# In the softmax step of pairs 5 and 0, the query tile with 128 keys is taken first of four instead of last

## Chip, core and metric

The kernel runs on one core of one Trainium2 chip, in one launch. The metric is the device time of that core in microseconds (us). All arithmetic of the kernel that matters here is 32-bit floating point.

## What is computed

One transformer block with modulation, for 2048 tokens of width 512. A causal attention with 16 heads of width 128 is followed by a mixture of 64 experts with 4 chosen for each token and two shared feed-forward units. Only the attention bears on the change:

```python
q = jnp.einsum('bpm,hmd->bphd', x, Q_w) + Q_b
k = jnp.einsum('bpm,hmd->bphd', x, K_w) + K_b
v = jnp.einsum('bpm,hmd->bphd', x, V_w) + V_b
logits = jnp.einsum('bqhd,bkhd->bhqk', q, k) / math.sqrt(d_head)
causal_mask = jnp.triu(jnp.ones((s, s), dtype=bool), k=1)
logits = jnp.where(causal_mask, NEG, logits)
scores = jax.nn.softmax(logits, axis=-1)
attn = jnp.einsum('bhqk,bkhd->bqhd', scores, v)
out = jnp.einsum('bqhd,hdm->bqm', attn, O_w) + O_b
```

Here `x` is the normalised and modulated input. The mask makes query tile number t (128 queries) need only the first (t+1)*128 keys, so the 16 query tiles of a head have widths from 128 to 2048 keys.

## The kernel before

**Steps.** The 16 query tiles of a head form 8 pairs: pair p holds the tiles 2p and 2p+1. `BATCHES` (L437) divides them into five steps s = 0 to 4: (7), (6), (5, 0), (4, 1), (3, 2). Steps 0 and 1 have two tiles each, steps 2, 3 and 4 have four. The list `steps` (L439) runs over all heads and steps, 80 in all. `tiles_of` (L450) gives the order of a step's tiles: in step 2 these are tile 11 (1536 keys), tile 1 (256), tile 10 (1408) and tile 0 (128).

**Softmax of one tile** (`softmax_tile`, L457). The tile is cut into chunks of at most 1024 keys. For each chunk `chunk` (L493) issues: matmuls of queries with keys into a PSUM tile `ps` (L500); on VectorE the causal mask on the last 128 columns of the tile (L512), the negated maximum (L513) and, for a second chunk, the minimum of both (L517); on ScalarE the exponential from `ps` into the probability tile `p`, with its row sum (L519, followed by an instruction that reads the accumulator), and for a second chunk a correction factor `fix` (L529). `ps` has two buffers (tag "sc" of the pool `psA`, L124), so a chunk's matmuls wait until the exponential of the chunk before the last one has read its buffer. The division by the sums, `normalise` (L471), is put off: it is flushed in the middle of the next chunk, or at the end of the step. In steps 2 to 4 its large part goes to ScalarE, after the next chunk's exponential (L714); in steps 0 and 1 it is done on VectorE (L487).

**From probabilities to values.** At a step's end `swap` (L727) flushes what was put off and issues 16 DMAs on SP's queue (L544), which move 32-row blocks of `p` to their transposed places in `pt`. Later VectorE transposes the 32x32 blocks in two halves (`turn`, L732, L554). Then TensorE multiplies with the values into a PSUM tile `po` (`weighted_values`, L572); every one of these matmuls reads both halves of `pt`. ScalarE adds the bias (`at`, L581), and GpSimd's queue stores the result (L586).

**The loop** (L746) runs over the 80 steps. Loop turn (hd, s) carries three streams, which `merge` (L83) interleaves by their share of work done: the softmax of the step two further on (first in the list, so it wins a tie), the weighted values of step s itself, and `fillers`: projections of the next head (`project`, L207, its matmuls at L217) in turns 0 to 2, values of the next group of heads (`make_v`, L419) in turns 3 and 4, and matmuls of the output (L688) in the last head. At 0.55 and 0.8 of the turn's work stand the two transposes for the next step:

```python
streams = [weighted_values(hd, s, turned.pop(n)), fill]
if n + 2 < len(steps):
    streams.insert(0, softmax_work(n + 2))
...
if n + 1 < len(steps):
    marks.append((0.55, lambda: turn(n + 1, 0)))
    marks.append((0.8, lambda: turn(n + 1, 1)))
merge([st for st in streams if st], marks)
if n + 2 < len(steps):
    swap(n + 2)
```

So the softmax of step 2 is worked on in loop turn (hd, 0); it follows on the softmax of step 1 in the turn before (of the head before), and the softmax of step 3 follows on it in turn (hd, 1). The order on each engine is the order of these calls; engines run their own instructions in order.

Of the kernel before, what the change touches and what calls it, by code (L numbers as in the profile page):

```python
# [23 lines left out]
def adaln_block_kernel(  # L24
# [96 lines left out]
    with ExitStack() as att:  # L121
# [328 lines left out]
        def tiles_of(s):  # L450

            prs = BATCHES[s]
            if len(prs) == 1:
                return [(prs[0], 1), (prs[0], 0)]
            return [(prs[0], 1), (prs[1], 1), (prs[0], 0), (prs[1], 0)]

        def softmax_tile(hd, s, pr, i, pb):  # L457
# [261 lines left out]
        def softmax_work(n):  # L719
            hd, s = steps[n]  # L720
            probs[n] = pp.tile([P, PW], F32, name="p")
            out = []
            for pr, i in tiles_of(s):
                out += softmax_tile(hd, s, pr, i, probs[n])
            return out
# [760 lines left out]
```

## Time and profile before

| what | us |
|---|---|
| three runs: lowest, median, highest | 2420.52, 2423.49, 2424.94 |
| the profiled execution: its time | 2422.97 |
| the profiled execution: its span, first to last instruction | 2421.2 |
| granted clock of TensorE, mean over the span | 0.996 of full speed |
| attention loop, about | 107 to 1695 of the span |
| one head, start of loop turn 0 to the next, heads 7 to 8 | 811.9 to 910.3 |
| DMAs that move `p` to `pt` (SP's queue): issue to landing, median | 2.2 |

Times of instructions that the change touches, as means over the kernel (ns): for a chunk of 128 keys the mask takes 290, the maximum 292, the exponential 363 and its read of the accumulator 194, the scaling by ScalarE 390. The mask and the maximum of a chunk of 384 keys take 290 and 558, its exponential 582; for 1024 keys the maximum takes 1213, the exponential 1115 and the scaling 1146. One half of a transpose takes 2242 for step 0, 1976 for step 1 and 1907 for steps 2 to 4.

A row of the timeline gives the start in the span, the time, the engine, the line, the operation, the tiles (output<-inputs), the shape and a count; consecutive instructions of a line are merged. In brackets stands how long the engine was idle before it, and which instruction released it. A matmul of the program makes two MATMUL records, each with a weight load on the row of PEld. The end of a MATMUL record includes its way through the array, so that at full flow the next one starts before it ends: records of 512 columns follow each other every 0.43 us, of 256 columns every 0.215, and the two of a 128-column matmul take 0.22 together.

### The profile page before, as it was taken

The numbers are of one execution on the slowest core, as the hardware profiler recorded it, in microseconds if no ns is written. First come the engines' busy times: TensorE is split into PE (matmuls) and PEld (weight loads), VectorE is DVE, ScalarE is ACT, GpSimd is POOL, SyncE is SP. The second block draws the span as 40 slices with busy tenths as digits, with TensorE's granted clock in tenths as the row PEclk, the third lists the DMA queues.
The fourth block names the chain that finished last, engine by engine and source line by source line (L and its number), as shares of the span: only waits on it lengthen the run. The fifth ranks groups of instructions, "written<-read, shape, count | busy, mean of one in ns | idle before, by whom it ended". The sixth has DMA issues, their size and how long they took to land. (4 is left out here: it accounts for less than half of the span.)

```text
span 2421.2 us, 26178 instructions
## 1 busy us (share of the span) xinstructions
PE 2362.5 (98%) x8406; PEld 1500.5 (62%) x8406; DVE 1513.2 (62%) x2878; ACT 829.8 (34%) x1737; POOL 219.2 (9%) x286
## 2 busy tenths in 40 slices
PE   7999999999999999999999999999999999999999
PEld 3566656666566665666656656555444476877743
DVE  5367666676676767767666666774655563654564
ACT  3243443444444444444444443432211221222200
POOL 0000000000000000000000000000000111111074
PEclk9999999999999999999999999999999999999999
DMA  4224444454454444444435445564432368877665
GB/s 139 64 71 116 120 118 109 98 143 102 101 127 105 117 120 96 114 111 103 112 93 129 110 99 120 164 194 134 152 122 87 98 203 246 236 217 240 191 194 158
DMA packets 223681, 325.22 MB, mean 134 GB/s; under 512 B 31876, under 2 KB 138424, under 8 KB 223544
## 3 DMA queue, kind: packets, MB, share of 16 engines
q1 hardware_dynamic: 196664, 252.21, 40.3%
q0 software_dynamic: 17664, 54.54, 7.5%
q10 hardware_dynamic: 9216, 16.78, 1.8%
q8 instruction: 68, 1.11, 0.2%
q14 instruction: 69, 0.57, 0.1%
HBM read 138.86 MB, written 41.94 MB: 75 GB/s over the span
## 5 line engine op out<-in xcount | busy, mean ns | idle before, releaser
L519 ACT ACTIVATE p<-ps,nm 128x1024 f32<-128x1024 f32 (+7 forms) x384 | 332.4, 866 | 885.1 <-DVE nm L517 403.9
L572 PEld LDWEIGHTS po<-pt,v 128*128 128x128 f32 x2304 | 426.5, 190 | 249.8 <-issue 187.8
L572 PE MATMUL po<-pt,v 128*128 128x256 f32 (+1 forms) x2304 | 572.3, 368 | 6.6 <-DVE pt L554 5.2
L500 PE MATMUL ps<-kt,qt 128*128 128x512 f32 (+3 forms) x1280 | 531.2, 531 | 20.9 <-ACT p L519 18.7
L513 DVE TENSOR_REDUCE nm<-ps 128x1 f32<-128x1024 f32 (+7 forms) x384 | 348.9, 909 | 48.9 <-PE ps L500 40.2
L554 DVE STREAM_TRANSPOSE pt<-pt 128x1664 f32<-128x1664 f32 (+2 forms) x160 | 318.0, 1988 | 56.3 <-DMA pt<-p 51.4
L500 PEld LDWEIGHTS ps<-kt,qt 128*128 128x128 f32 x1280 | 234.7, 190 | 180.9 <-issue 137.0
L427 PE MATMUL pv<-wv,hT 128*128 128x256 f32 x1024 | 240.8, 379 | 2.2 <-ACT v L434 2.2
L586 POOL DMA_DIRECT2D atd<-at x128 | 74.4, 584 | 1617.4 <-ACT at L581 1155.8
L427 PEld LDWEIGHTS pv<-wv,hT 128*128 128x128 f32 x1024 | 194.4, 190 | 31.2 <-ACT v L434 3.0
L714 ACT ACTIVATE p<-p,rs 128x1024 f32<-128x1024 f32 (+7 forms) x256 | 200.5, 807 | 6.2 <-DVE rs L475 5.9
L1056 PE MATMUL pso<-hT,T 128*128 128x512 f32 x384 | 174.8, 600 | 0.0
L217 PE MATMUL pqk<-T,sw 128*128 128x512 f32 x360 | 169.2, 592 | 0.0
L512 DVE TENSOR_TENSOR ps<-ps,causal 128x128 f32<-128x128 f32 x256 | 74.3, 290 | 150.0 <-PE ps L500 147.6
L1348 PE MATMUL pse<-wgu,xbT 128*128 128x256 f32 x512 | 121.1, 379 | 0.0
L1056 PEld LDWEIGHTS pso<-hT,T 128*128 128x128 f32 x384 | 70.1, 192 | 72.1 <-issue 71.3
L217 PE MATMUL pqk<-hT,wq 128*128 128x512 f32 x240 | 114.1, 598 | 0.0
L1265 PE MATMUL psd<-wsd,hs 128*128 128x512 f32 x256 | 111.5, 592 | 0.0
L1348 PEld LDWEIGHTS pse<-wgu,xbT 128*128 128x128 f32 x512 | 93.8, 190 | 11.7 <-issue 1.0
L217 PEld LDWEIGHTS pqk<-T,sw 128*128 128x128 f32 x360 | 68.3, 190 | 47.8 <-issue 43.0
L1331 POOL DMA_INDIRECT xb<-h2d,tok x64 | 65.2, 1018 | 301.8 <-PE tpx L1341 275.1
L1343 ACT COPY xbT<-tpx 128x512 f32<-128x512 f32 x64 | 37.4, 586 | 146.0 <-DVE y L1371 54.4
(365 smaller groups left out, 2344.3 us busy)
## 6 DMA issues: line engine op xcount, KB each, us to landing
pt<-p SPq DMA_DIRECT2D x768, 104.0 KB, 2.2
pt<-p SPq DMA_DIRECT2D x256, 124.0 KB, 2.3
pt<-p SPq DMA_DIRECT2D x256, 108.0 KB, 2.2
atd<-at POOLq DMA_DIRECT2D x128, 128.0 KB, 2.2
wgu<-in_L_ffn_Wg_dram SPq DMA_DIRECT2D x64, 256.0 KB, 4.6
wgu<-in_L_ffn_Wu_dram SPq DMA_DIRECT2D x64, 256.0 KB, 4.9
wd<-in_L_ffn_Wd_dram SPq DMA_DIRECT2D x64, 256.0 KB, 3.7
ybd<-y ACTq DMA_DIRECT2D x64, 256.0 KB, 3.8
```

Of the source, the lines that this page charges most:

```text
L217: nc.tensor.matmul(out=ps, lhsT=l[:, k], rhs=r[:, k], start=(k == 0), stop=(k == 1))
L427: nc.tensor.matmul(out=ps, lhsT=hTs[t // 4][:, k, (t % 4) * P : (t % 4 + 1) * P], rhs=wv[:, k].rearrange("p i d -> p (i d)"), start=(k == ...
L500: nc.tensor.matmul(out=ps[:, o : o + wo], lhsT=q, rhs=kts[hd, (c0 + o) // 512][:, :wo], start=True, stop=True,)
L513: nc.vector.tensor_reduce(nm[:, n : n + 1], ps[:, :w], AX.X, ALU.max, negate=True)
L519: nc.scalar.activation(rows[:, r0 + c0 // P : r0 + (c0 + w) // P], ps[:, :w].rearrange("q (r b k) -> q r b k", b=4, k=32), AF.Exp, bias=nm ...
L554: nc.vector.transpose(part, part)
L572: nc.tensor.matmul(out=po if wide else po[:, P:], lhsT=vts[g, kt // 4][:, kt % 4, hh * DH : (hh + 1) * DH], rhs=rows[:, r : r + last + 1 : ...
L586: nc.gpsimd.dma_start(out=atd[hd, :, o * 256 : (o + 1) * 256], in_=at[:, m])
L714: nc.scalar.activation(part, part, AF.Identity, scale=r)
L1056: nc.tensor.matmul(out=ps, lhsT=abs_[pr][:, hd, i * P : (i + 1) * P], rhs=wos[hd // 4][:, hd % 4, :], start=(hd == 0), stop=(hd == H - 1),)
L1265: nc.tensor.matmul(out=ps, lhsT=hsh[b, f][:, i * P : (i + 1) * P], rhs=wsd[:, f, :], start=(f == 0), stop=(f == NHC - 1),)
L1348: nc.tensor.matmul(out=ps, lhsT=xts[e][:, k, :], rhs=weights[e][:, k].rearrange("p i h -> p (i h)"), start=(k == 0), stop=(k == DC - 1),)
```

## The change

`tiles_of` gets a case of its own for the step whose second pair is pair 0:

```diff
             prs = BATCHES[s]
             if len(prs) == 1:
                 return [(prs[0], 1), (prs[0], 0)]
+            if prs[1] == 0:
+                return [(0, 0), (prs[0], 1), (0, 1), (prs[0], 0)]
             return [(prs[0], 1), (prs[1], 1), (prs[0], 0), (prs[1], 0)]
```

Step 2 of every head then takes its tiles in the order 0, 11, 1, 10. Its chunks had the widths 1024, 512, 256, 1024, 384, 128 and now have 128, 1024, 512, 256, 1024, 384. The places of the tiles in `p` and `pt` stay (`first_block`, L443), and so do all other steps. No instruction is added or removed; the merge spreads them otherwise. At the start of turn (hd, 0) TensorE's order was (512-column projections count two matmuls)

```
ps 1024 | po 256 | projection x2 | po x3 | projection x2 | po | ps 512 | po x2
```

and becomes

```
ps 128 | po 256 | projection x2 | ps 1024 | po x3 | projection x2 | po x2 | ps 512 | po
```

and at its end `ps 384 | po 256 | ps 128 | po 128`, followed by `ps 1024` of the next step, becomes `ps 384 | po 256 | po 128`, followed by the same. In the last head, whose filler is the output's matmuls, the 1024 chunk stands after one `po` and one such matmul. The order of SP's and GpSimd's instructions is the same as before. On ScalarE `at` (L581) stood between the scalings of tile 10 and of tile 0; it now stands ahead of the scalings of tile 10, which are the last before the swap.

## Prediction

> **What bounds the kernel now.** I read the page's busy shares first, then the list of who waited for whom on TensorE, then the timeline at the two places where the order changes.
>
> ```profile
> PE 2362.5 (98%) x8406; PEld 1500.5 (62%) x8406; DVE 1513.2 (62%) x2878; ACT 829.8 (34%) x1737; POOL 219.2 (9%) x286
> ```
>
> TensorE is busy 98% of the span and no matmul is added or removed, so the time can change only through TensorE's gaps. The waits of TensorE (total us, times, longest) name two kinds in the attention loop:
>
> ```profile
> PE ps L500 <- ACT p L519: 18.7, 18, 1.6
> PE po L572 <- DVE pt L554: 5.2, 4, 3.6
> ```
>
> Fifteen of the 18 waits of the first kind lie at one place, which I call border A: the start of loop turn (hd, 1), heads 0 to 14. In head 7 the timeline shows:
>
> ```profile
> 831.24 0.81 PE L500 MATMUL ps<-kt,qt 128*128 128x384 f32 x2
> ...
> 832.31 0.38 PE L500 MATMUL ps<-kt,qt 128*128 128x128 f32 x2
> ...
> 832.53 0.39 PE L572 MATMUL po<-pt,v 128*128 128x128 f32 x2
> ...
> 833.20 0.58 ACT L519 ACTIVATE p<-ps,nm 128x384 f32<-128x384 f32 x1 [3.29 <-DVE nm L517]
> ...
> 833.93 1.98 PE L500 MATMUL ps<-kt,qt 128*128 128x512 f32 x4 [1.01 <-ACT p L519]
> ```
>
> The two last chunks of step 2 (384 and 128 keys) are issued 1.07 us apart. The next chunk, 1024 keys of step 3, needs the buffer of the 384 chunk, and that is free only at 833.93, 0.15 after its exponential ends. Nothing else stands behind it that TensorE could do.
>
> The second place is border B, the start of turn (hd, 0), where the changed step begins. Before, in head 7:
>
> ```profile
> 809.84 2.24 DVE L554 STREAM_TRANSPOSE pt<-pt 128x1984 f32<-128x1984 f32 x1
> ...
> 811.88 1.88 PE L500 MATMUL ps<-kt,qt 128*128 128x512 f32 x4
> 812.00 0.27 DVE L512 TENSOR_TENSOR ps<-ps,causal 128x128 f32<-128x128 f32 x1
> ...
> 813.41 0.80 ACT L519 ACTIVATE p<-ps,nm 128x640 f32<-128x640 f32 x1 [3.12 <-DVE nm L517]
> 813.60 0.59 PE L572 MATMUL po<-pt,v 128*128 128x256 f32 x2
> ```
>
> The first po matmul needs the second transpose of pt, which ends at 812.08, **after** TensorE has entered the turn at 811.88. There is no wait, because the 1024 chunk lies between and covers 1.72 us. Where the transpose is later still, the wait shows (head 0, then head 13):
>
> ```profile
> 113.08 1.09 PE L572 MATMUL po<-pt,v 128*128 128x256 f32 x2 [3.63 <-DVE pt L554]
> ...
> 1403.92 0.70 PE L572 MATMUL po<-pt,v 128*128 128x256 f32 x2 [0.21 <-DVE pt L554]
> ```
>
> **Part 1, removed: the wait at border A.** With the new order the chunk before the last one has 1024 keys (tile 10); its exponential in head 7 ran from 828.31 to 829.42, over 3 us before TensorE reaches the border. The 384 chunk's buffer is wanted only by the second chunk of the turn, in head 7 at 841.34. The price of one wait: in full flow the 1024 chunk would have started 0.22 after 832.53, at 832.75; it started at 833.93, 1.18 late, and took 1.82 to the next row instead of 1.72, so 1.28 lost. The same over heads 0 to 14: 1.28, 1.80, 1.27, 1.51, 1.28, 1.28, 1.92, 1.28, 1.34, 1.27, 1.88, 1.32, 1.32, 1.75, 1.28. Sum **-21.8**. Head 15 has no such wait (its output matmuls lie between). Next in line at the border is the po matmul after the 1024 chunk; its transpose ended 0.5 to 1.3 before the border in all 15 heads, so nothing is late there.
>
> **Part 2, added: the transpose loses its cover at border B.** Now only a 128 chunk (0.22) stands ahead of the first po. Let S be the start of turn (hd, 0) and T the end of the second transpose. T - S in heads 1 to 14: 0.84, 0.47, 1.51, 0.99, 0.63, 0.45, 0.20, 1.38, 0.64, 0.87, 0.47, 1.65, 2.04, 0.94; sum 13.1. po starts 0.055 after T (head 13: 1403.87 to 1403.92) and its restart costs 0.10 (0.53 to the next row, where full flow has 0.43). So each head loses T - S + 0.055 - 0.22 + 0.10: 13.1 - 14 x 0.065 = 12.2. Off go the 0.47 and 0.09 that heads 13 and 12 lost there already: **+11.6**. Behind the waiting po on TensorE's queue stands everything, the projections and the 1024 chunk included; VectorE and ScalarE wait for these but are behind TensorE here anyway, still scaling step 1 until 816.38.
>
> **Part 3, the moved 1024 chunk.** It now needs the buffer of step 1's last chunk (640 keys). That exponential starts 1.33 after T, takes 0.80, and frees the buffer 0.15 later: T + 2.28. TensorE arrives at T + 0.055 + 0.53 + 1.72 = T + 2.305. A tie; a weight load is issued ahead of its matmul and waits with it, so I take one restart, 0.1 x 14 = **+1.4** (nothing at best; 0.3 each at worst).
>
> **Part 4, head 15 and head 0.** In head 15 T - S is 2.42 and only one po and one output matmul (0.86) stand ahead of the 1024 chunk. Lost: 2.42 - 0.065 = 2.36 for po, then T + 2.28 against T + 1.445 = 0.83 and a restart, less the 0.86 lost there now: **+2.4**. In head 0 both transposes stand ahead of the loop, and the 1024 chunk that TensorE did meanwhile now comes after: 1.72 - 0.22 = **+1.5**. [...] The row: the gap of 3.63 was followed by a granted clock of half speed,
>
> ```profile
> 110.00:115.00 5.00, 1.92 (x4) 1.23 (x5) 4.14 (x3) 0.78 (x1) 0.00 (x0) 0.83 0.76 176
> ```
>
> (the 0.83 is the clock; four projection records took 3.22 instead of 1.88). [...] The gap here becomes 5.1. [...]
>
> **Part 5, hidden.** The tile's own instructions (on VectorE 0.29 + 0.29 + 0.16, on ScalarE 0.36 + 0.19 + 0.39) move from the end to the start. At the start they lie behind step 1's scaling; the 1024 chunk's maximum moves from 816.29 to about 817.0, its exponential to about 818.3, and the buffers it frees are wanted after 822. If that cover were gone, 0.7 a head would show, 11 in all. At the end `at` now precedes tile 10's scaling on ScalarE; it needs the last po, done at about 833, and the scaling cannot start before 834.7 anyway. The swap's 16 DMAs on SP start about 3.2 after the 384 chunk's exponential starts (1.53 to the scaling, 1.66 for it), at 836.6 instead of 837.1: earlier on the clock, but 0.8 later against TensorE, which gained 1.28. They take 10.06 to issue and 2.2 to land, until about 848.9; the second transpose that needs them stood at 850.74, behind work that follows TensorE, and moves to 849.5. Covered, except in the five heads with the longest waits (0.1 to 0.2 each), where the wait behind it at turn (hd, 2) grows: **+0.5** (0 to 3).
>
> **Sum.** -21.8 + 11.6 + 1.4 + 2.4 + 1.5 + 0.5 = -4.4. Against the profiled execution's own 2422.97 (span 2421.2 and 1.8 around it) that gives 2418.6. The median of the runs is 0.5 above the profiled one, so 2419.
>
> **The rivals.** (a) *The full gain.* The transpose keeps its distance to TensorE rather than to the start of the turn, or the new waits are half as long: then -12 to -18, 2405 to 2411. For it: VectorE follows TensorE most of the time. Against: ahead of the second transpose VectorE is backed up (maximum, step 0's scaling of 1.28, transpose, with hardly a pause), and in heads 3 and 12 the first transpose waits some 2 us for its DMAs, so TensorE can't pull it. (b) *Slower: the wait at border B outgrows the one at A.* Place: the second transpose of step 0's pt. Price: 14 times the wait. It decides from a mean of about 1.25 a head at B, where I have 0.83 + 0.1. For it: the four latest heads (1.51, 1.65, 2.04, 2.42) have a mean of 1.9; if DMA arrivals were as late in every head, part 2 would be 14 x 1.84 = 25.8, and the whole about +10: 2433. Against: eight of the 14 stay under 0.9. (c) *It doesn't do what it says*: the 1024 chunk at border A meets another wait of the same size; then only the added parts count, +17: 2441. Against it stands the 3 us margin.
>
> **How the numbers follow.** Forecast (both waits trade, net -10 to +3) 0.63; (a) 0.15; (b) 0.19; (c) 0.03. Three runs spread 0.18%, so about 0.2%, 4.8 us, is what can be told from no change. The forecast's own range is 2413 to 2426, from parts 2 to 5 each at their ends; it sits just inside the 0.2%, and divides into 0.27 faster, 0.34 same, 0.02 slower. With (a) faster, (b) and (c) slower mostly and the same in some: 0.42, 0.36, 0.22. The range that should hold 8 in 10 reaches towards (a) and (b): 2410 to 2428.
>
> **What would show it.** Right: the list of waits has "ps <- ACT p" down from 18 entries to a few, none at border A, and "po <- DVE pt" up from 4 to about 16, some 15 us, all at the start of turn (hd, 0). Part 3 is wrong if ps waits at border B by more than 0.2. Part 5 is wrong if turn (hd, 2) opens with longer waits than now. The forecast falls if T - S has another mean than 0.9, or if a clock below 1.00 shows in the loop outside head 0.

## The result, and the profile after

The changed kernel takes 2420.05 us (median of 20 runs, 2418.85 to 2427.73) against 2425.63 for the kernel before (20 runs, 2420.52 to 2428.93). The ratio is 0.9982, with a 95% interval of 0.9976 to 0.9988: a small gain of 0.18%, some 4.4 us (2.9 to 5.8 by the interval; the two medians lie 5.6 apart). The profiled execution has a span of 2418.1 us.

The page's first row and the list of who waited on TensorE (total us, times, longest), after the change, whose lines are two further down in the file (L502 is L500 of before, L574 is L572, L556 is L554):

```profile
PE 2363.9 (98%) x8406; PEld 1500.2 (62%) x8406; DVE 1511.8 (63%) x2878; ACT 828.8 (34%) x1737; POOL 217.8 (9%) x286
```

```profile
PE po L574 <- DVE pt L556: 15.0, 12, 5.1
...
PE ps L502 <- ACT p L521: 4.0, 8, 0.9
```

The two waits have changed places: `ps` for the exponential fell from 18.7 to 4.0, `po` for the transpose rose from 5.2 to 15.0. The busy times of TensorE, VectorE and ScalarE are the same within 0.2%.

At border A (start of turn (hd, 1)) in head 7, the timeline after:

```profile
828.93 0.81 PE L502 MATMUL ps<-kt,qt 128*128 128x384 f32 x2
...
829.58 0.82 PE L574 MATMUL po<-pt,v 128*128 128x256 f32 x4
...
830.23 1.88 PE L502 MATMUL ps<-kt,qt 128*128 128x512 f32 x4
...
830.90 0.58 ACT L521 ACTIVATE p<-ps,nm 128x384 f32<-128x384 f32 x1 [3.29 <-DVE nm L519]
```

The next step's first chunk starts at 830.23, before the exponential of the 384 chunk has begun, and with no idle time. At border B (start of turn (hd, 0)), head 1:

```profile
210.80 2.24 DVE L556 STREAM_TRANSPOSE pt<-pt 128x1984 f32<-128x1984 f32 x1
...
211.72 0.39 PE L502 MATMUL ps<-kt,qt 128*128 128x128 f32 x2
...
213.09 0.70 PE L574 MATMUL po<-pt,v 128*128 128x256 f32 x2 [0.99 <-DVE pt L556]
...
214.38 0.80 ACT L521 ACTIVATE p<-ps,nm 128x640 f32<-128x640 f32 x1 [3.83 <-DVE nm L519]
...
215.32 0.30 PEld L502 LDWEIGHTS ps<-kt,qt 128*128 128x128 f32 x2 [0.64 <-ACT p L521]
215.35 1.96 PE L502 MATMUL ps<-kt,qt 128*128 128x512 f32 x4
```

The 128 chunk is over in 0.22 us, the transpose ends at 213.04, and po starts 0.05 later. The 640 exponential ends at 215.18. The weight load of the 1024 chunk is held back until 215.32, and its first matmul starts at 215.35, on time; but the four matmuls take 1.79 to the next row instead of 1.72, so 0.07 is lost.

**Where the time went, head by head.** Some VectorE additions of the projections start as soon as TensorE delivers their input (the one of L252 in head 7 0.04 us after the projection's last record ends, before the change and after); they come in the same order in both kernels, so the difference of their times shows where one kernel gains on the other. Each step below is corrected by 0.22 for the 128 chunk, which is done earlier in the turn.

| place | forecast, us | measured, us |
|---|---|---|
| border A, heads 0 to 14 | -21.8 | -21.8 (1.27 to 1.91 each) |
| border B, heads 1 to 14 (parts 2 and 3) | +13.0 | +11.2 (0.07 to 1.98 each; 1.0 of the sum is part 3) |
| border B, head 15 | +2.4 | +2.4 |
| border B, head 0 | +1.5 | +1.5 |
| start of turn (hd, 2) | +0.5 | +2.0 (heads 4, 8, 9, 13) |
| sum | -4.4 | -4.7 |

From here on "the loop" is the time from the first `ps` matmul to the first matmul of the last head's output (L1035 before, L1037 after): 1637.7 us before, 1632.6 after, so 5.1 less. The 0.4 that the rows leave over is a wait that only the trace before has, in turn (15, 0): an output matmul (L688) waits there for `hT`, and 0.34 and a restart of 0.10 are lost.

```profile
1605.80 1.13 PE L688 MATMUL psb<-hT,T 128*128 128x512 f32 x2 [0.18 <-DVE hT L657]
```

The loop is used for the experiments because it leaves out what lies behind it: that part took 729 us in the profile before, 731 in the profile after (where the clock stood at half speed for 6.8 us from 1707.5 on, against 3.4 us in the same place before), and 736 to 748 in the profiles of the experiments, which ran on other chips, where the kernel before had medians of 2437 to 2439. The ratios, from all executions of a kernel, stand in the table at the end of the experiments; a loop time is that of one profiled execution.

### The profile page after: what moved, and what is told of

Its sections match the earlier page's. It is cut to its first block, busy times and chain, and to the rows that moved or that the text cites. A ratio compares the mean times of both kernels' runs of the same rounds, so it can differ in the third digit from the quotient of the medians.

```text
span 2418.1 us, 26181 instructions
## 1 busy us (share of the span) xinstructions
PE 2363.9 (98%) x8406; PEld 1500.2 (62%) x8406; DVE 1511.8 (63%) x2878; ACT 828.8 (34%) x1737; POOL 217.8 (9%) x286
## 3 DMA queue, kind: packets, MB, share of 16 engines
q8 instruction: 68, 1.11, 0.2%
## 5 line engine op out<-in xcount | busy, mean ns | idle before, releaser
L574 PE MATMUL po<-pt,v 128*128 128x256 f32 (+1 forms) x2304 | 571.1, 368 | 16.7 <-DVE pt L556 15.0
L574 PEld LDWEIGHTS po<-pt,v 128*128 128x128 f32 x2304 | 426.6, 190 | 254.5 <-issue 184.1
L502 PE MATMUL ps<-kt,qt 128*128 128x512 f32 (+3 forms) x1280 | 530.9, 531 | 5.8 <-ACT p L521 4.0
L515 DVE TENSOR_REDUCE nm<-ps 128x1 f32<-128x1024 f32 (+7 forms) x384 | 347.5, 908 | 36.1 <-PE ps L502 27.3
L556 DVE STREAM_TRANSPOSE pt<-pt 128x1664 f32<-128x1664 f32 (+2 forms) x160 | 317.8, 1987 | 54.5 <-DMA pt<-p 53.7
L502 PEld LDWEIGHTS ps<-kt,qt 128*128 128x128 f32 x1280 | 233.7, 190 | 172.6 <-issue 137.8
```

Source lines behind the costliest of these rows:

```text
L502: nc.tensor.matmul(out=ps[:, o : o + wo], lhsT=q, rhs=kts[hd, (c0 + o) // 512][:, :wo], start=True, stop=True,)
L515: nc.vector.tensor_reduce(nm[:, n : n + 1], ps[:, :w], AX.X, ALU.max, negate=True)
L556: nc.vector.transpose(part, part)
L574: nc.tensor.matmul(out=po if wide else po[:, P:], lhsT=vts[g, kt // 4][:, kt % 4, hh * DH : (hh + 1) * DH], rhs=rows[:, r : r + last + 1 : ...
```

## The experiments

**The 128 tile second instead of first.** Does the gain at border A come without the price at border B?

```diff
-                return [(0, 0), (prs[0], 1), (0, 1), (prs[0], 0)]
+                return [(prs[0], 1), (0, 0), (0, 1), (prs[0], 0)]
```

> Order of step 2: tile 11, tile 0, tile 1, tile 10 (chunks 1024, 512, 128, 256, 1024, 384). My theory (the change removes the wait of the 1024 chunk at the start of turn (hd, 1), worth 21.8 us, and pays for it with the transpose that loses its cover at the start of turn (hd, 0)): the end of the step is that of the changed kernel, the start that of the kernel before, so the gain stays and the price goes. 2425.6 - 21.8 + about 2 for longer waits at turn (hd, 2) = about 2405, ratio 0.992; po waits for pt fall from 15.0 us back to about 5, ps waits for p stay at about 4. Rival (the two waits are one slack that moves about, TensorE runs ahead of VectorE and has to wait somewhere): 2415 to 2420, the wait turns up elsewhere.

The loop took 1626.2 us: 11.5 less than before, where the theory had about 20. Border A was free of waits and po waits for pt were back at 5.1, as expected. But a wait of 0.35 (0.62 lost, by the two neighbouring rows) appeared in heads 0 to 14, in the middle of the step. Head 7:

```profile
818.41 0.82 PE L502 MATMUL ps<-kt,qt 128*128 128x128 f32 x4
...
819.50 0.37 ACT L521 ACTIVATE p<-ps,nm 128x128 f32<-128x128 f32 x1 [1.68 <-DVE nm L515]
...
820.01 1.98 PE L502 MATMUL ps<-kt,qt 128*128 128x512 f32 x4 [0.35 <-ACT p L521]
```

The first row merges the 128 and the 256 chunk. The 1024 chunk of tile 10 needs the buffer of the 128 chunk, and only 0.86 us of matmuls lie between. So both theories were partly right: the price of border B is separate and can be avoided, but here the small chunk makes a wait of the same kind wherever it is a near neighbour. The error was mine: I had looked at the two borders only.

**The cover put back at border B.** The changed kernel, with the projections ahead of the weighted values in turn (hd, 0):

```diff
                 streams = [weighted_values(hd, s, turned.pop(n)), fill]
+                if s == 0:
+                    streams.reverse()
```

> The changed kernel, but in turns (hd, 0) the fillers stand ahead of the weighted values in the merge, so that two projection matmuls (1.72 us) lie between the 128 chunk and the first po. My theory: two waits lie one behind the other at this border, the transpose (T) and the exponential of the 640 chunk (T + 2.28), which the 1024 chunk needs. With the cover back the first goes, and TensorE reaches the 1024 chunk at S + 2.37 instead of after the wait, so it waits there for about the same time: T - S + 0.01 a head. Time about 2420, the same as the changed kernel within 2 us; po waits for pt fall from 15.0 to about 7, ps waits for p rise from 4.0 by about 10. Rival (only the transpose counts): 2409, no new wait of ps.

The loop took 1632.0 us, 0.6 less than with the changed kernel. In head 3, where the transpose was late (it ends at 411.83, and TensorE entered the turn at 410.62):

```profile
412.56 0.59 PE L574 MATMUL po<-pt,v 128*128 128x256 f32 x2
...
413.17 0.79 ACT L521 ACTIVATE p<-ps,nm 128x640 f32<-128x640 f32 x1 [3.83 <-DVE nm L519]
...
414.10 1.98 PE L502 MATMUL ps<-kt,qt 128*128 128x512 f32 x4 [0.94 <-ACT p L521]
```

po no longer waits, and the 1024 chunk waits instead, until 0.14 after the 640 exponential. Heads 1 to 14 lost 12.6 us at this border, where the changed kernel lost 11.9 (not counting what was lost before the change). Over the run, po for pt fell from 15.0 to 5.4 and ps for p rose from 4.0 to 13.1. Two waits stand one behind the other here, with nearly the same due time; removing the visible one gains nothing.

**The small tiles of two steps in the middle.** As the first experiment, and step 3 too:

```diff
+            if prs[1] == 1:
+                return [(prs[0], 1), (1, 0), (1, 1), (prs[0], 0)]
```

> As e1, and step 3 in the order tile 9, tile 2, tile 3, tile 8 (chunks 1024, 256, 384, 512, 1024, 128). My theory: the same kind of wait (0.27 + 0.1 us a head, up to 1.0 in some) at the start of turn (hd, 2), where 128 and 384 were the last two chunks, goes too: 15 x 0.37 + 2 = 7 less than e1, about 2398 to 2400; ps waits for p near 1 us. Rival (the later swap of step 3, whose last scaling is now that of 1024 + 128 columns, makes the transposes of turn (hd, 3) late): no better than e1, with po waits for pt or longer DMA waits of the transposes in turn (hd, 3).

The loop took 1620.4, 5.7 less than the first experiment, where 7 were expected. At the start of turn (hd, 2) 7.2 us went: 0.38 in most heads, and more in heads 4, 7, 8 and 9, as the theory had it. In head 0 0.9 came back, because the clock stayed at half speed twice as long (mean clock 0.66 from 110 to 120 us, against 0.83 in the first experiment). The row of ps for p still has 4.4 us, the new waits between chunks of step 2, where about 1 was expected. The later swap of step 3 did no harm.

**The transpose later.** The changed kernel, with step 0's second transpose at 0.95 of turn (hd, 4):

```diff
-                    marks.append((0.8, lambda: turn(n + 1, 1)))
+                    marks.append((0.95 if s == 4 else 0.8, lambda: turn(n + 1, 1)))
```

> The changed kernel, with the second transpose of step 0 at 0.95 of turn (hd, 4) instead of 0.8; it then stands on VectorE behind the maximum of the 640 chunk and ends at about S + 3.1 in every head instead of S + 0.2 to S + 2.4. My theory (each head loses T - S - 0.07 there): 14 x 3.0 = 42 instead of 11, so about 30 us more than the changed kernel, 2450, and no ps wait at that border (the 640 exponential is now early). Rival (the cost at that border is the restart and the order of the matmuls, not the end of the transpose): within 5 us of the changed kernel.

The loop took 1690.5, 58 more than with the changed kernel, where 30 were expected. The wait is the same in heads 1 to 14, 3.02 or 3.03 us, so the end of the transpose sets it, as the theory says: 14 x 3.29 lost (3.19 by the rows, and the restart) is 46, 34 more than the changed kernel lost there (11.9). Most of the rest is the clock. The timeline of head 7, and a row of a stretch: its bounds, its length, the busy times of PE, PEld, VectorE, ScalarE and GpSimd with their instructions, then the granted clock, the share of the DMA engines and GB/s:

```profile
835.17 0.72 PE L574 MATMUL po<-pt,v 128*128 128x256 f32 x2 [3.02 <-DVE pt L556]
...
835.70 3.58 PE L217 MATMUL pqk<-hT,wq 128*128 128x512 f32 x4
```

```profile
835.00:840.00 5.00, 4.83 (x9) 2.24 (x10) 2.25 (x8) 1.14 (x3) 0.76 (x2) 0.66 0.44 119
```

A clock of 0.66 over 5 us is half speed for 3.4 us, and the four projection records took 3.58 instead of 1.88. In 16 us behind the border the clock read 0.89 in eleven of the 14 heads and 1.00 in heads 1, 6 and 12, whose wait was the same. At 1.7 us each that is 19, and 34 + 19 = 53 of the 58. Head 15 has 3.4 of what is left (0.5 of wait and 2.9 of clock), head 0 1.0 (clock), the start of turn (hd, 2) 0.6.

**The order 11, 1, 0, 10.** A test of the spacing as a rule with numbers:

```diff
-                return [(prs[0], 1), (0, 0), (0, 1), (prs[0], 0)]
+                return [(prs[0], 1), (0, 1), (0, 0), (prs[0], 0)]
```

> Order of step 2: tile 11, 1, 0, 10 (chunks 1024, 512, 256, 128, 1024, 384). In e1 a wait of 0.35 on the page (0.62 lost) turned up in each head where the 1024 chunk of tile 10 came two chunks after the 128 chunk. Theory now: any chunk waits when the matmuls between the end of the chunk two before it and its own start take less than the time from that chunk's matmuls to the end of its exponential (about 1.6 us for 256 keys, 2.0 for 384). Here only 0.43 + 0.22 us of matmuls lie between the 256 chunk and the 1024 chunk of tile 10, so about 1.1 us a head is lost there, 0.5 more than in e1: the attention loop takes 1626 + 7 = 1633 us, about as long as with the changed kernel (1632.6); ps waits for p about 12 us. Rival (e1's wait comes from the 128 chunk as such, its short matmuls): the same loss as in e1, 1626.

The loop took 1632.85; 1633 was expected. The wait of the 1024 chunk was 0.79 or 0.80 in heads 0 to 14 (0.96 lost and the restart), and ps for p 14.6 us in all, against 12 expected. Head 7:

```profile
821.02 0.59 PE L502 MATMUL ps<-kt,qt 128*128 128x256 f32 x2
...
821.88 0.38 PE L502 MATMUL ps<-kt,qt 128*128 128x128 f32 x2
823.06 1.98 PE L502 MATMUL ps<-kt,qt 128*128 128x512 f32 x4 [0.80 <-ACT p L521]
```

The 128 chunk's own shortness is not the cause: here the wait is for the 256 chunk's exponential.

**The order 11, 0, 10, 1.** The 256 tile last:

```diff
-                return [(prs[0], 1), (0, 0), (0, 1), (prs[0], 0)]
+                return [(prs[0], 1), (0, 0), (prs[0], 0), (0, 1)]
```

> Order of step 2: tile 11, 0, 10, 1 (chunks 1024, 512, 128, 1024, 384, 256). By the same theory the middle has no wait (3.2 us of matmuls between the 512 chunk and the second 1024 chunk), and at the start of turn (hd, 1) 1.5 us lie between the end of the 384 chunk and the next 1024 chunk, against 0.87 in the kernel before, so half of the old wait comes back: 0.6 a head, attention loop about 1627, the same as e1, with ps waits for p of about 0.4 x 15 at that border only. Rival (the wait at that border is made by the 128 chunk being last): 1618, no wait there.

The loop took 1638.1, no better than before, and 11 more than expected. The middle had no wait, as foretold (but for 0.4 us in head 3), but border A lost 1.11 to 2.76 a head instead of 0.6, and in head 1, where the wait was longest (2.49), the clock then fell to half speed and cost 1.7 more. Head 7:

```profile
830.72 1.96 DVE L556 STREAM_TRANSPOSE pt<-pt 128x1728 f32<-128x1728 f32 x1
...
831.84 0.81 PE L502 MATMUL ps<-kt,qt 128*128 128x384 f32 x2
...
832.60 0.65 DVE L248 TENSOR_TENSOR kt<-kt,pqk 128x512 f32<-128x512 f32 x1
833.17 0.29 DVE L514 TENSOR_TENSOR ps<-ps,causal 128x128 f32<-128x128 f32 x1
...
835.01 1.98 PE L502 MATMUL ps<-kt,qt 128*128 128x512 f32 x4 [0.84 <-ACT p L521]
```

The 384 chunk now comes early enough to fall behind the second transpose on VectorE: its matmuls are done by 832.65, but its mask starts at 833.17, after a transpose and an addition. That delay explains about 0.5 us; why heads 1, 10 and 11 lost more (2.76, 2.11, 1.66) stays open. I had taken the time from a chunk's matmuls to its free buffer as fixed (2.0 us). It is that only if VectorE is free.

**More matmuls behind each small chunk.** The order of before, untouched; a chunk of fewer than 512 keys counts as 512 when the merge spreads the work:

```diff
-            return [(min(SC, width - n * SC), lambda n=n: chunk(n)) for n in range(nch)]
+            return [(max(512, min(SC, width - n * SC)), lambda n=n: chunk(n)) for n in range(nch)]
```

> The kernel before, its order of tiles untouched, but a chunk of fewer than 512 keys counts as 512 in the merge, so that more other matmuls follow it. Theory (the whole loss is one of spacing): 3.4 us of matmuls lie between the 384 chunk and the next step's first chunk, and as much between the 128 chunk of step 3 and the chunk after the next; the waits at the starts of turns (hd, 1) and (hd, 2) both go, 21.8 + 5.5 us, and the 1024 chunk still covers the transpose at the start of turn (hd, 0). Attention loop 1610 against 1637.7, ratio about 0.989; ps waits for p under 2 us, po waits for pt about 5. Rival (VectorE, with the transposes now behind the masks and maxima of the small chunks, becomes late): po waits for pt at turns (hd, 1) and (hd, 2), and no gain over e3 (1620).

The loop took 1610.95: 26.7 less than before, for 27.3 worked out: the waits of turns (hd, 1) and (hd, 2) that went come to 27.8, and the clock in head 0 took 1.0 back, as in the experiment with the two steps. This is the version that beats both kernels: 2410.02 us (4 runs) against 2437.42 of the kernel before, ratio 0.9881 (0.9865 to 0.9898). In the list of TensorE's waits ps for p is down to the last row here; the first three rows are of other kinds:

```profile
PE pmr L309 <- DMA wm<-in_L_wmod_dram: 7.2, 1, 7.2
PE psg L1119 <- DVE sig L1108: 6.5, 1, 6.5
PE po L572 <- DVE pt L554: 5.5, 4, 3.6
...
PE ps L500 <- ACT p L519: 0.4, 1, 0.4
```

Border A, head 7:

```profile
817.57 0.81 PE L500 MATMUL ps<-kt,qt 128*128 128x384 f32 x2
...
819.71 0.58 ACT L519 ACTIVATE p<-ps,nm 128x384 f32<-128x384 f32 x1 [2.52 <-DVE nm L517]
...
821.67 1.88 PE L500 MATMUL ps<-kt,qt 128*128 128x512 f32 x4
```

4.1 us now lie between the starts of the 384 chunk and of the chunk after the next (2.7 before, of which 1.2 was the wait), and its exponential ends 1.4 before the border.

**The same floor in the changed kernel.**

> The changed kernel with the same floor of 512 in the merge. Theory: the wait at the start of turn (hd, 0) depends on the transpose and the cover in front of it alone and stays (po waits for pt about 15 us); the waits at turn (hd, 2) go (5.5 + 2 us). Attention loop 1632.6 - 7 = 1625, 15 more than e10: that difference is the price of the lost cover, measured by itself. Rival (the price of the changed order is one of spacing as well): within 5 us of e10.

The loop took 1628.0, 4.5 less than the changed kernel and 17.1 more than the experiment above. po for pt was 18.5 us and ps for p had gone from the waits at turn (hd, 2). So the price of the lost cover is there whatever the spacing: 16.2 of the 17.1 are waits at the start of turn (hd, 0), against 11.2 + 2.4 + 1.5 = 15.1 by the ledger of the changed kernel. The other 1.0 is the clock. In head 12 it fell to half speed after a wait of 1.98 us and cost 1.8, while head 0 lost 0.8 less to it than in the experiment above:

```profile
1294.68 0.81 PE L574 MATMUL po<-pt,v 128*128 128x256 f32 x2 [1.98 <-DVE pt L556]
```

```profile
1295.13:1298.54 3.41, 3.41 (x6) 1.42 (x5) 2.08 (x7) 1.65 (x4) 0.64 (x1) 0.50 0.00 0
```

| kernel | loop, us | ratio to before | interval |
|---|---|---|---|
| before | 1637.7 | 1 | |
| changed | 1632.6 | 0.9982 | 0.9976 to 0.9988 |
| 128 second | 1626.2 | 0.9944 | 0.9931 to 0.9958 |
| cover put back | 1632.0 | 0.9974 | 0.9961 to 0.9987 |
| two steps | 1620.4 | 0.9920 | 0.9906 to 0.9933 |
| transpose later | 1690.5 | 1.0196 | 1.0181 to 1.0212 |
| 11, 1, 0, 10 | 1632.9 | 0.9980 | 0.9970 to 0.9990 |
| 11, 0, 10, 1 | 1638.1 | 0.9996 | 0.9988 to 1.0005 |
| floor of 512, old order | 1611.0 | 0.9881 | 0.9865 to 0.9898 |
| floor of 512, new order | 1628.0 | 0.9943 | 0.9926 to 0.9959 |

## Why the prediction was right, point by point

- **Part 1** held: no wait took the old one's place at border A. The 21.8 agree to the tenth because both are read from the trace before; what was at stake was that nothing else was due there.
- **Part 2**: T - S before gave 11.6; measured at border B in heads 1 to 14, without part 3, 10.2. The mechanism held, and the sum held better than its heads, which is partly luck: T - S fell from 2.04 to 0.54 in head 13 and from 0.98 to 0.20 in head 4, where the second transpose had waited 1.43 and 0.68 for its DMAs before the change and did not after, and it rose by about 0.5 in heads 1 and 3. The mean went from 0.93 to 0.84. The experiment with the late transpose shows the dependence by itself; the two with the floor show that the price stays when the spacing is mended.
- **Part 3** called a tie and charged one restart a head, 1.4. It came as described, a little cheaper: the weight load of the 1024 chunk waits for the 640 exponential (the row at 215.32 above), and 0.07 is lost in each of the 14 heads, 1.0 in all. The limit lies just there, as the experiment with the cover put back shows.
- **Part 4**: head 15 and head 0 as worked out. After the longer gap of 5.13 us in head 0 the clock read 0.85 and 0.81 in the two stretches of 5 us, together 3.4 us at half speed, as before the change. The upper end of the forecast's range holds 1.7 us for a second fall of the clock in head 0; that was my estimate, and no run shows the 1.7. From 110 to 120 us the mean clock is 0.83 here, but 0.66 with the same gap of 5.1 us in the runs of the late transpose and of the floor in the changed kernel, and also 0.66 with the old gap of 3.6 us in the runs of the two steps and of the floor in the old order; that cost those runs 0.2 to 1.0 us. The other new waits, 2.08 us at most, left the clock at 1.00 here; their length alone did not assure that, since a wait of 1.98 us was followed by half speed in another run (last section).
- **Part 5** had the right mechanism and too small a size: 2.0 instead of 0.5, and, but for head 13, in other heads than those with the longest waits. The swap starts 3.27 after the 384 exponential, as said; but in heads 4 and 9 the second transpose then waited 0.81 and 0.74 for its DMAs, where I had counted it covered; that is 1.5 of the 2.0. Head 9, timeline of the kernel before, where the transpose follows the addition without a wait, and of the changed kernel:

```profile
1046.36 0.69 DVE L231 TENSOR_TENSOR qt<-p__6126,pqk 128x512 f32<-128x512 f32 x1 [0.92 <-PE pqk L217]
1046.96 1.91 DVE L554 STREAM_TRANSPOSE pt<-pt 128x1664 f32<-128x1664 f32 x1
```

```profile
1042.35 0.69 DVE L231 TENSOR_TENSOR qt<-p__6126,pqk 128x512 f32<-128x512 f32 x1 [0.92 <-PE pqk L217]
...
1043.78 1.91 DVE L556 STREAM_TRANSPOSE pt<-pt 128x1664 f32<-128x1664 f32 x1 [0.74 <-DMA pt<-p]
...
1047.60 1.98 PE L502 MATMUL ps<-kt,qt 128*128 128x512 f32 x4 [0.82 <-ACT p L521]
```

- **The rivals.** The full gain (a) did not come: the transpose did not follow TensorE, and border B lost 11.2. The slower case (b) needed a mean above 1.25 us at border B and met 0.80. Case (c) is excluded by the clean border A.

The sum, -4.4, met -4.4 by the ratio and -5.1 in the loop. The agreement of the first two to the tenth is luck: the ratio's interval runs from -2.9 to -5.8, the errors of parts 2 and 3 (-1.8) and of part 5 (+1.5) nearly cancel, and the 0.4 in head 15 was in no part.

## What to carry to other kernels

With two buffers, a chunk waits for the exponential of the chunk two before it (1.01 us at border A in head 7 of the kernel before): what counts is the work that lies between, so give a small chunk as much other work behind it as a larger one has, rather than move it. The time from a chunk's matmuls to its free buffer is not fixed either: it grew by about 0.5 us in the order 11, 0, 10, 1, where the chunk fell behind a transpose on VectorE. Before moving a large piece of work away from a place (1.72 us of matmuls here), look at what it covers there, and at what is due just behind that, since a second wait may stand in its shadow (0.94 us in head 3 with the cover put back). Where the gain and the price of a change are of one size, as here, look whether the cause (here the spacing) can be treated by itself.

## What the runs showed of the hardware

A wait of 3.02 or 3.03 us on TensorE in heads 1 to 14 of the late transpose was followed by a granted clock of 0.50 for 3.41 us in eleven of them, and not in heads 1, 6 and 12. In the traces before and after the change the stretches at half speed last 3.41 or 6.83 us (but for the last, which the end of the run cuts off), and they begin whole multiples of 3.413 us apart; with the late transpose, those in heads 2 and 3 begin at 316.89 and 422.70, which is 31 x 3.413. Rows with that spacing, around the wait in head 7, then in head 1:

```profile
832.31:835.72 3.41, 0.55 (x3) 0.50 (x4) 3.06 (x7) 1.65 (x4) 1.03 (x2) 1.00 0.00 0
835.72:839.13 3.41, 3.41 (x6) 1.34 (x5) 1.63 (x4) 0.46 (x2) 0.04 (x1) 0.50 0.49 137
...
211.08:214.49 3.41, 2.29 (x12) 1.54 (x10) 2.60 (x6) 1.11 (x4) 0.00 (x0) 1.00 0.00 0
214.49:217.90 3.41, 1.51 (x5) 0.98 (x6) 3.31 (x6) 1.13 (x4) 1.07 (x2) 1.00 0.22 76
217.90:221.31 3.41, 3.41 (x12) 1.87 (x11) 1.43 (x4) 1.04 (x3) 0.00 (x0) 1.00 0.45 103
```

In head 7 nearly the whole wait falls into one row, in which TensorE is busy for 0.55 us, and in the next row the clock reads 0.50. In head 1 the border of two rows cuts the wait; TensorE is busy for 2.29 and 1.51, and the clock reads 1.00. In heads 6 and 12 the wait is cut in the same way (2.05 and 1.72; 1.98 and 1.80).

So the length of a wait alone does not decide. One of 2.08 us (head 15 of the changed kernel; 1.56 busy in its row) left the clock at 1.00; one of 2.49 (order 11, 0, 10, 1, head 1) and one of 1.98 (floor of 512, new order, head 12; 1.44 busy) were followed by half speed. A wait of 3 us behind which the clock fell cost about 5.0 in all (3.29 and 1.7).
